# Sparse graph attention: the destination's gathered score accumulates in PSUM onto the source's columns

## The chip, the cores and the metric

The kernel runs on one core of one Trainium2 chip. The metric is the device time of one execution in microseconds; lower is better. The whole network below is one program of some 50,000 instructions, and the change touches one stage of it.

## The reference, cut to what matters

The network takes 3125 node vectors of 256 numbers and two edge lists, and runs two rounds of a graph layer beside an attention layer, each followed by a mixture of experts. The stage that matters is the gate of the first mixture. It is a graph attention (four heads with four numbers each) over 65,536 random edges whose ends are numbers below 4096 (a source beyond the last node counts as the last node, an edge with a destination beyond it drops out), and its result weighs four experts that all nodes run through.

```python
h = (x_flat @ W_gat).reshape(M, HEADS, NUM_EXPERTS)
a_src = (h * att_src).sum(-1)                 # four scores per node
a_dst = (h * att_dst).sum(-1)
e = leaky_relu(a_src[src] + a_dst[dst], negative_slope=0.2)
e_max = segment_max(e, dst)                   # the self loops are among src, dst
ee = exp(e - e_max[dst])
alpha = ee / (segment_sum(ee, dst)[dst] + 1e-16)
agg = segment_sum(h[src] * alpha[:, :, None], dst).reshape(M, 16) + b_gat
scores = layernorm(agg).reshape(M, HEADS, NUM_EXPERTS).mean(1)
# top two of the four scores, softmax over them, and the experts' outputs are weighed by it
out = sum(g[ei] * (gelu(x @ W1[ei] + b1[ei]) @ W2[ei] + b2[ei]) for ei in range(4))
```

The softmax needs a shift per destination, and any shift that is the same for all edges of a destination gives the same result. The kernel takes the self loop's score in place of the maximum, where the scores are near enough to zero (`NEAR`), and has another path, `in_full`, for other data.

## The kernel before, in words

**Buckets.** Earlier stages have sorted the edges into chunks of 128 places. There are 25 destination tiles of 128 nodes, and each has 30 chunks (`CHUNKS`), ordered by the tile of the source node: 750 chunks in all. `low_d` in DRAM holds for each place the low seven bits of the destination (row 0) and of the source (row 1).

**A step.** `sparse()` is a generator that works through the chunks six at a time (`SOME`), 125 steps, and it has four parts:

- `fetched` (L1520) loads the low bits of six chunks, broadcast over 128 partitions, into `hot` (four buffers; L1524), and VectorE turns them into one-hot columns by a comparison with the partition's number (L1525).
- `gathered` (L1535) multiplies, for each chunk, the source one-hot by a table of the source tile (`tables[0]`: 20 columns a node, four `att_s` scores and 16 numbers `hg`, each split into three bfloat16 parts that add up to the float32 value; L1540) and the destination one-hot by a table of the destination tile (`tables[1]`: eight columns a node, four `att_d` scores and four self-loop scores, in three parts; L1542). Both results stand side by side in `pg` (six chunks by three parts by 28 columns of PSUM, two buffers), and VectorE adds the three parts into `vs` (L1544).
- `weighed` (L1547) runs once for two steps, on 12 chunks. VectorE adds the destination's score to the source's (L1550), applies the leaky rectifier (L1551), and subtracts the self-loop score (L1552); ScalarE takes the exponential (L1553); VectorE multiplies the 16 numbers by it (L1555); ScalarE and GpSimd split the result into three bfloat16 parts, `mp3` (L1558 to L1561).
- `put_of` (L1528) builds the destination one-hots the other way round (`put`, three buffers, VectorE, L1531), and `added` (L1566) multiplies them with `mp3` into `acc`, one bank that collects the 30 chunks of a destination tile (L1571); ScalarE copies it to `got` (L1574).

**What runs beside it.** The steps are drawn from the generator while experts 1 and 2, and the last group of expert 0, run: after each output tile of an expert (`keep_beside`, L1608), `each1` = 2.6 steps on average are emitted. An expert's part is a pair of float32 matmuls for each of four hidden blocks (`experts_hidden`, L284) with a Gelu on ScalarE (L287), then four float32 matmuls and a bias row for each of up to four row tiles (`expert`, L1418, L1419), and a ScalarE copy of the result to SBUF (L1611).

**The order.** Each engine runs its instructions in the order that the framework's scheduler has laid down beforehand, by its own model of costs and from the dependencies and the pools' buffer counts. What stands next to what on TensorE, VectorE and ScalarE is therefore decided by it and not by the source alone, and a change of one instruction can move others.

**Before and after the stage.** The groups ahead of it normalise, transpose and project the nodes and run expert 0; the tables are built from `node` and `goal` (L1499 to L1507). After it come the totals (L1629 to L1636), a branch to `in_full`, and expert 3 with the weighing of all four.

Of the kernel before, what the change touches and what calls it, by code (L numbers as in the profile page):

```python
# [8 lines left out]
F32 = mybir.dt.float32  # L9
BF16 = mybir.dt.bfloat16  # L10
I32 = mybir.dt.int32
AF = mybir.ActivationFunctionType
OP = mybir.AluOpType
# [4 lines left out]
P = 128  # L18
N = 3125
D = 256  # L20
NT = 25
# [31 lines left out]
HIS = 25  # L53
# [15 lines left out]
SOME = 6  # L69
# [34 lines left out]
def tile_gps(ctx: ExitStack, tc: tile.TileContext, a, out):  # L104
    nc = tc.nc
    V, S, G, T = nc.vector, nc.scalar, nc.gpsimd, nc.tensor
# [1279 lines left out]
    with ExitStack() as st:  # L1386
# [2 lines left out]
        V.memset(agg, 0.0)  # L1389
        node = fp.tile([P, NT, 20], F32, name="node", tag="node")  # L1390
        V.memset(node, 0.0)
        att_s, hg = node[:, :, 0:4], node[:, :, 4:20]
        goal = fp.tile([P, NT, 8], F32, name="goal", tag="goal")
        att_d = goal[:, :, 0:4]
        xT = xnT
# [27 lines left out]
        with ExitStack() as st2:  # L1423
# [74 lines left out]
            V.scalar_tensor_tensor(self_e, self_e, 0.2, self_e, op0=OP.mult, op1=OP.max)  # L1498
            tables = []  # L1499
            for nm, x, n in (("tabs", node, 20), ("tabd", goal, 8)):  # L1500
                tab = xp.tile([P, NT, 3, n], BF16, name=nm, tag=nm)
                rest = xp.tile([P, NT, n], F32, name=f"{nm}_r", tag="tabr", bufs=1)
                S.activation(tab[:, :, 0, :], x, AF.Copy)
                V.tensor_tensor(rest, x, tab[:, :, 0, :], op=OP.subtract)
                S.activation(tab[:, :, 1, :], rest, AF.Copy)
                V.tensor_tensor(tab[:, :, 2, :], rest, tab[:, :, 1, :], op=OP.subtract)
                tables.append(tab.rearrange("p t k v -> p t (k v)"))  # L1507
            over = buckets.over
            far = small.tile([P, 2], F32, name="far", tag="far")
            V.tensor_reduce(far[:, 0:1], att_s, axis=AX.XY, op=OP.max)  # L1510
# [23 lines left out]

            def gathered(at, vs, k0, n, hot):  # L1535

                pg = ps.tile([P, SOME, 3, 28], F32, name="pg", tag="pg", bufs=2)
                for j in range(n):
                    dh, k = (k0 + j) // CHUNKS, (k0 + j) % CHUNKS
                    T.matmul(pg[:, j, :, 0:20], lhsT=hot[:, 1, j * P:(j + 1) * P],  # L1540
                             rhs=tables[0][:, min(k, HIS - 1)], start=True, stop=True)
                    T.matmul(pg[:, j, :, 20:28], lhsT=hot[:, 0, j * P:(j + 1) * P],  # L1542
                             rhs=tables[1][:, dh], start=True, stop=True)
                V.tensor_reduce(vs[:, at:at + n], pg[:, :n].rearrange("p j k v -> p j v k"), axis=AX.X, op=OP.add)  # L1544
                return k0, n, at

            def weighed(vs, n):  # L1547
                vs = vs[:, :n]
                e = vs[:, :, 0:4]
                V.tensor_tensor(e, e, vs[:, :, 20:24], op=OP.add)  # L1550
                V.scalar_tensor_tensor(e, e, 0.2, e, op0=OP.mult, op1=OP.max)  # L1551
                V.tensor_tensor(e, e, vs[:, :, 24:28], op=OP.subtract)  # L1552
                S.activation(e, e, AF.Exp)  # L1553
                m = vs[:, :, 4:20].rearrange("p j (h v) -> p j h v", h=4)
                V.tensor_tensor(m, m, e[:, :, :, None].to_broadcast([P, n, 4, 4]), op=OP.mult)  # L1555
                mp3 = xp.tile([P, 2 * SOME, 3, 20], BF16, name="mp3", tag="mp3", bufs=4)
                rest = xp.tile([P, 2 * SOME, 20], F32, name="mrest", tag="mrest", bufs=1)
                S.activation(mp3[:, :n, 0], vs[:, :, 0:20], AF.Copy)  # L1558
                G.tensor_tensor(rest[:, :n], vs[:, :, 0:20], mp3[:, :n, 0], op=OP.subtract)
                S.activation(mp3[:, :n, 1], rest[:, :n], AF.Copy)  # L1560
                G.tensor_tensor(mp3[:, :n, 2], rest[:, :n], mp3[:, :n, 1], op=OP.subtract)  # L1561
                return mp3
# [13 lines left out]
            def sparse():  # L1576
# [5 lines left out]
                for i, k0 in enumerate(left):  # L1582
                    nx = fetched(left[i + 1], min(SOME, n - left[i + 1])) if i + 1 < len(left) else None
                    if not i % 2:
                        vs = xp.tile([P, 2 * SOME, 28], F32, name="vs", tag="vs", bufs=2)
                    done.append(gathered(SOME * (i % 2), vs, *x))
                    if i % 2 or not nx:
                        m = weighed(vs, sum(d[1] for d in done))
                        todo += [(m, *d) for d in done]
                        done = []  # L1590
                    if ready:
                        added(*ready.pop(0))
                    if len(todo) > 3:
                        ready.append(put_of(*todo.pop(0)))
                    x = nx
                    yield
# [30 lines left out]
            for _ in beside1:  # L1627
                pass
            tot = xp.tile([P, NT, 20], F32, name="tot", tag="tot")  # L1629
            V.tensor_reduce(tot, got.rearrange("p t (k v) -> p t v k", k=3), axis=AX.X, op=OP.add)  # L1630
            den = tot[:, :, 0:4]
            V.tensor_scalar(den, den, 1.0, 1e-16, op0=OP.add, op1=OP.add)
            V.reciprocal(den, den)
            V.tensor_tensor(tot[:, :, 4:20], tot[:, :, 4:20], hg, op=OP.add)
            V.tensor_tensor(agg.rearrange("p t (h e) -> p t h e", e=4), tot[:, :, 4:20].rearrange("p t (h e) -> p t h e", e=4),
                            den[:, :, :, None].to_broadcast([P, NT, 4, 4]), op=OP.mult)  # L1636

        def in_full(ap, ps):
# [626 lines left out]
```

## Time and profile before

| | us |
|---|---|
| Median of the timed runs | 3667.17 |
| Lowest and highest of three | 3664.85, 3675.57 |
| The profiled execution's own time | 3698.38 |
| Its span in the profile | 3696.6 |
| TensorE matmul busy in the span | 3477.4 (94%) |
| VectorE busy | 1912.1 (52%) |
| ScalarE busy | 1117.6 (30%) |
| GpSimd busy | 915.9 (25%) |
| The stage of the sparse attention: first `pg` matmul to last `acc` matmul | 1915.0 to 2235.5 |

How to read it: the share of an engine is a mean over stages with different limits, and so the stage's own busy times are looked at below. PE is TensorE's matmuls, PEld its weight loads, DVE is VectorE, ACT ScalarE, POOL GpSimd, and SP the queue that issues most transfers. Matmuls are pipelined, so that a row of the profile is longer than the turn that the matmul takes on the engine; L1540 is line 1540 of the kernel. The profiled execution is one, with a time of its own; the times are from other executions.

### The profile page before, as it was taken

The page shows a single profiled execution, that of the slowest core. Times are in us where ns is not written, and L with a number is a line of the kernel's source. Part 1 is how long each engine was busy: PE and PEld are TensorE (multiplying, and loading weights), DVE is VectorE, ACT ScalarE, POOL GpSimd, SP SyncE. Part 2 cuts the span into 40 slices and gives each one's busy share as a digit, 9 for nine tenths or more (in the row PEclk, how much of TensorE's full clock was granted, in tenths as well). Part 3 has the DMA queues.
Part 4 walks back from the last instruction along what each step waited for, and adds up shares of the span by engine and source line. Part 5 has one row for each costly group of instructions (what it writes and reads, how often), then busy time and mean ns, then how long its engine had stood idle before and what let it go on. Part 6 is the DMA issues. An engine that isn't in the chain of part 4 may idle for free. (4 is left out here: it accounts for less than half of the span.)

```text
span 3696.6 us, 50192 instructions
## 1 busy us (share of the span) xinstructions
PE 3477.4 (94%) x18153; PEld 2114.0 (57%) x18153; DVE 1912.1 (52%) x6827; ACT 1117.6 (30%) x2092; POOL 915.9 (25%) x915
## 2 busy tenths in 40 slices
PE   6999999989999899899899898999999999999998
PEld 3666566656566566544466665564444544444687
DVE  8757767777677687110529888761023032223421
ACT  5433433334333443200346774320023000000233
POOL 0044325532455066000003232100024010000244
PEclk9999899999999899999999999999999999999999
DMA  7013525541456276522666661103211222221576
GB/s 216 18 39 43 66 42 55 63 73 32 49 58 65 64 92 71 142 87 87 205 187 167 177 183 52 47 12 115 82 37 47 72 66 61 60 61 51 154 185 154
DMA packets 347439, 326.89 MB, mean 88 GB/s; under 512 B 143792, under 2 KB 311497, under 8 KB 345751
## 3 DMA queue, kind: packets, MB, share of 16 engines
q1 hardware_dynamic: 212503, 280.87, 29.4%
q10 hardware_dynamic: 105424, 26.40, 7.8%
q0 software_dynamic: 29232, 16.09, 2.6%
q8 instruction: 151, 2.47, 0.3%
q14 instruction: 129, 1.06, 0.1%
HBM read 239.75 MB, written 90.83 MB: 89 GB/s over the span
## 5 line engine op out<-in xcount | busy, mean ns | idle before, releaser
L431 POOL DMA_INDIRECT btab<-b_word,b_key x512 | 535.2, 1045 | 674.3 <-PE mm L284 294.2
L1192 PE MATMUL ag<-chb,Hb 128*128 128x512 bf16 (+1 forms) x1800 | 420.8, 388 | 3.8 <-issue 3.8
L1192 PE MATMUL ag<-chb,xb 128*128 128x512 bf16 (+2 forms) x1950 | 401.5, 366 | 10.1 <-DMA xb<-xb_d 5.4
L284 PE MATMUL mm<-hT,w 128*128 128x512 f32 (+1 forms) x896 | 386.6, 570 | 2.0 <-ACT hid L287 1.4
L1092 PE MATMUL o<-w,hid 128*128 128x256 f32 (+1 forms) x1600 | 387.1, 390 | 0.0
L1092 PEld LDWEIGHTS o<-w,hid 128*128 128x128 f32 (+1 forms) x1600 | 293.8, 190 | 54.0 <-issue 14.3
L1192 PEld LDWEIGHTS <-xb 128*128 128x128 bf16 (+1 forms) x2100 | 183.8, 98 | 226.9 <-issue 17.2
L287 ACT ACTIVATE hid<-mm,fm 128x512 f32<-128x512 f32 (+1 forms) x336 | 210.4, 630 | 328.3 <-PE mm L284 326.4
L1192 PEld LDWEIGHTS <-Hb 128*128 128x128 bf16 (+1 forms) x2100 | 184.8, 99 | 217.3 <-issue 25.4
L284 PEld LDWEIGHTS mm<-hT,w 128*128 128x128 f32 x896 | 163.2, 201 | 143.5 <-issue 124.9
L1418 PE MATMUL o<-f0w,hid 128*128 128x256 f32 (+1 forms) x800 | 215.4, 398 | 3.7 <-ACT hid L287 3.7
L950 PE MATMUL mm<-wqkv,hT 128*128 128x512 f32 (+1 forms) x400 | 205.6, 639 | 9.0 <-DVE kmax L961 5.7
L284 PE MATMUL mm<-xnT,f0w 128*128 128x512 f32 (+1 forms) x448 | 204.6, 582 | 4.6 <-issue 4.0
L475 DVE SCALAR_TENSOR_TENSOR b_junk<-kr,b_key,b_tri 128x128 bf16<-128x128 f32 x512 | 175.4, 343 | 33.7 <-DMA kr<-keys_g 31.5
L1809 POOL DMA_INDIRECT slots<-rb,r_ati x50 | 49.4, 987 | 505.3 <-DVE rb L1802 399.8
L732 ACT ACTIVATE g_st<-gc 128x400 bf16<-128x400 f32 x192 | 93.5, 500 | 242.8 <-PE gc L728 239.6
L1418 PEld LDWEIGHTS o<-f0w,hid 128*128 128x128 f32 (+1 forms) x800 | 141.0, 190 | 40.1 <-issue 13.9
L2147 DVE TENSOR_TENSOR a2T<-a2T,ag 128x512 f32<-128x512 f32 x24 | 15.9, 688 | 277.8 <-PE ag L1192 277.7
L719 DVE TENSOR_TENSOR g_ol<-g_all,g_lo 128x1024 bf16<-128x1024 bf16 (+1 forms) x199 | 136.3, 685 | 35.8 <-PE gc L728 34.7
L728 PEld LDWEIGHTS <-g_ol 128*128 128x128 bf16 (+1 forms) x1589 | 119.1, 164 | 61.7 <-issue 42.7
L232 ACT ACTIVATE hT<-tr,fm 128x512 f32<-128x512 f32 (+1 forms) x126 | 85.5, 719 | 159.7 <-PE tr L230 158.4
L1936 POOL DMA_INDIRECT out_dram<-yo,dest x56 | 87.5, 1562 | 186.2 <-DMA out_dram<-yo,dest 78.7
(505 smaller groups left out, 5691.5 us busy)
## 6 DMA issues: line engine op xcount, KB each, us to landing
hot<-low_d SPq DMA_DIRECT2D x125, 384.0 KB
kr<-keys_g SPq DMA_DIRECT2D x256, 128.0 KB
f1w<-in_f_w_dram SPq DMA_DIRECT2D x56, 512.0 KB
slots<-blank SPq DMA_DIRECT2D x14, 1950.0 KB
A<-g_st ACTq DMA_DIRECT2D x24, 800.0 KB
chb<-A SPq DMA_DIRECT2D x48, 397.2 KB
chb<-A SPq DMA_DIRECT2D x48, 384.0 KB
chb<-A SPq DMA_DIRECT2D x120, 128.0 KB
```

The costliest lines, as they stand in the source:

```text
L284: pace[0] = T.matmul(ph[:, :n], lhsT=w1[:, k, hb * P:(hb + 1) * P], rhs=xT[:, k, :n], start=(k == 0), stop=(k == 1))
L287: S.activation(h[:, :n], ph[:, :n], AF.Gelu, bias=bias[hb])
L431: d = G.indirect_dma_start(out=btab.rearrange("(n o) -> n o", o=1), out_offset=bass.IndirectOffsetOnAxis(ap=self.key[:, c:c + 1].bitcast(I ...
L475: ranked = V.scalar_tensor_tensor(junk, kr[:, (j % EACH) * P:(j % EACH + 1) * P], self.key[:, c0 + j:c0 + j + 1], self.tri, op0=OP.is_equa ...
L719: V.tensor_tensor(lo[:r, :, :k], self.all[:r, :, :k], self.lo[:r, None, c:c + k].to_broadcast([r, P, k]), op=OP.is_equal)
L728: T.matmul(p[:, j, :], lhsT=lo[:r, :, j], rhs=hi[:r, j, :h], start=True, stop=True)
L732: S.activation(stage.rearrange("p h (l j) -> p h l j", l=2)[:, :, :, j0:j0 + k], p.rearrange("p j (l h) -> p h l j", l=2), AF.Copy)
L950: pace[0] = T.matmul(pqk[:r], lhsT=hT[:, k, j * P:j * P + r], rhs=wqkv[:, k, 0:512], start=(k == 0), stop=(k == 1))
L1092: pace[0] = T.matmul(po[:r], lhsT=hid[hb][:, j * P:j * P + r], rhs=w2[:, hb, :], start=(hb == 0), stop=False)
L1192: T.matmul(acc[fb, g][:, :n], lhsT=Xb[:r, s, i, fb * P:(fb + 1) * P], rhs=ch[:r, at:at + n], start=first, stop=last, skip_group_check=g == ...
L1418: T.matmul(po[:r], lhsT=hid[hb][:, j * P:j * P + r], rhs=w2[:, hb, :], start=(hb == 0), stop=False)
L1936: d = G.indirect_dma_start(out=out, out_offset=bass.IndirectOffsetOnAxis(ap=dest[:, c:c + 1], axis=0), in_=yo[:, c, :], in_offset=None, bo ...
```

## The change

In `pg`, and so in `vs`, the 28 columns of a chunk become 24. The columns are reordered so that the 16 numbers come first, then the four source scores. The source table is padded with four zero columns to 24 and cleared by a memset, so that the first matmul writes 72 contiguous columns and opens the accumulation. The second matmul, with the destination's eight columns, accumulates onto columns 16 to 23 of each of the three parts: its four scores add to the source's scores, and its four self-loop scores add to the zeros. The addition on VectorE in `weighed` is left out. All else is renumbering.

```diff
-        att_s, hg = node[:, :, 0:4], node[:, :, 4:20]
+        hg, att_s = node[:, :, 0:16], node[:, :, 16:20]
...
-                tab = xp.tile([P, NT, 3, n], BF16, name=nm, tag=nm)
+                whole = xp.tile([P, NT, 3, n + n % 8], BF16, name=nm, tag=nm)
+                tab = whole[:, :, :, 0:n]
+                if n % 8:
+                    V.memset(whole, 0.0)
...
-                tables.append(tab.rearrange("p t k v -> p t (k v)"))
+                tables.append(whole.rearrange("p t k v -> p t (k v)"))
...
-                pg = ps.tile([P, SOME, 3, 28], F32, name="pg", tag="pg", bufs=2)
+                pg = ps.tile([P, SOME, 3, 24], F32, name="pg", tag="pg", bufs=2)
                 for j in range(n):
                     dh, k = (k0 + j) // CHUNKS, (k0 + j) % CHUNKS
-                    T.matmul(pg[:, j, :, 0:20], lhsT=hot[:, 1, j * P:(j + 1) * P],
-                             rhs=tables[0][:, min(k, HIS - 1)], start=True, stop=True)
-                    T.matmul(pg[:, j, :, 20:28], lhsT=hot[:, 0, j * P:(j + 1) * P],
-                             rhs=tables[1][:, dh], start=True, stop=True)
+                    T.matmul(pg[:, j], lhsT=hot[:, 1, j * P:(j + 1) * P],
+                             rhs=tables[0][:, min(k, HIS - 1)], start=True, stop=False)
+                    T.matmul(pg[:, j, :, 16:24], lhsT=hot[:, 0, j * P:(j + 1) * P],
+                             rhs=tables[1][:, dh], start=False, stop=True)
                 V.tensor_reduce(vs[:, at:at + n], pg[:, :n].rearrange("p j k v -> p j v k"), axis=AX.X, op=OP.add)
...
-                e = vs[:, :, 0:4]
-                V.tensor_tensor(e, e, vs[:, :, 20:24], op=OP.add)
+                e = vs[:, :, 16:20]
                 V.scalar_tensor_tensor(e, e, 0.2, e, op0=OP.mult, op1=OP.max)
-                V.tensor_tensor(e, e, vs[:, :, 24:28], op=OP.subtract)
+                V.tensor_tensor(e, e, vs[:, :, 20:24], op=OP.subtract)
                 S.activation(e, e, AF.Exp)
-                m = vs[:, :, 4:20].rearrange("p j (h v) -> p j h v", h=4)
+                m = vs[:, :, 0:16].rearrange("p j (h v) -> p j h v", h=4)
...
-                        vs = xp.tile([P, 2 * SOME, 28], F32, name="vs", tag="vs", bufs=2)
+                        vs = xp.tile([P, 2 * SOME, 24], F32, name="vs", tag="vs", bufs=2)
...
-            den = tot[:, :, 0:4]
+            den = tot[:, :, 16:20]
...
-            V.tensor_tensor(tot[:, :, 4:20], tot[:, :, 4:20], hg, op=OP.add)
+            V.tensor_tensor(tot[:, :, 0:16], tot[:, :, 0:16], hg, op=OP.add)
```

More of the change, by code (lines that the diff above doesn't have):

```diff
@@ L1630, in tile_gps @@
             V.tensor_reduce(tot, got.rearrange("p t (k v) -> p t v k", k=3), axis=AX.X, op=OP.add)
-            den = tot[:, :, 0:4]
+            den = tot[:, :, 16:20]
             V.tensor_scalar(den, den, 1.0, 1e-16, op0=OP.add, op1=OP.add)
             V.reciprocal(den, den)
-            V.tensor_tensor(tot[:, :, 4:20], tot[:, :, 4:20], hg, op=OP.add)
-            V.tensor_tensor(agg.rearrange("p t (h e) -> p t h e", e=4), tot[:, :, 4:20].rearrange("p t (h e) -> p t h e", e=4),
+            V.tensor_tensor(tot[:, :, 0:16], tot[:, :, 0:16], hg, op=OP.add)
+            V.tensor_tensor(agg.rearrange("p t (h e) -> p t h e", e=4), tot[:, :, 0:16].rearrange("p t (h e) -> p t h e", e=4),
                             den[:, :, :, None].to_broadcast([P, NT, 4, 4]), op=OP.mult)
```

## Prediction

> **What bounds the kernel now.** I read the page's slices first, then the busy time of the stage that the change touches, then its groups of instructions, its waits, and two strips of the timeline. The span is 3696.6 us, and TensorE is busy almost throughout.
>
> ```profile
> PE   6999999989999899899899898999999999999998
> DVE  8757767777677687110529888761023032223421
> ```
>
> The edited code runs in one stage, from 1915 us (the first `pg` matmul) to 2235 us (the last `acc` matmul): slices 21 to 24, where both PE and DVE are high. Its stretches (columns: length, then busy us and count for PE, PEld, DVE, ACT, POOL, then clock, DMA share, GB/s):
>
> ```profile
> 1950.00:2050.00 100.00, 95.21 (x977) 62.82 (x976) 92.62 (x214) 66.74 (x130) 31.67 (x42) 1.00 0.69 169
> 2050.00:2200.00 150.00, 134.58 (x1361) 90.82 (x1360) 127.79 (x295) 106.84 (x190) 45.64 (x59) 0.95 0.65 177
> sum 317.00, PE 289.98 PEld 193.94 DVE 269.74 ACT 218.34 POOL 93.72; mean PE 72.49 PEld 48.49 DVE 67.43 ACT 54.58 POOL 23.43
> ```
>
> The sum is over 1915 to 2232. DVE is busy 269.7 of 317 us, 93% in the first 100 us shown and 85% in the next 150. PE shows 290, but a matmul's row is longer than its turn on the engine. These strips show turns as the distance between starts (the first strip is the edited code, the second a later stage with 53 and 512 columns):
>
> ```profile
> 2021.04 0.19 PE L1540 MATMUL pg<-tabs,hot 128*128 128x60 bf16 x1
> 2021.07 0.17 PE L1542 MATMUL pg<-tabd,hot 128*128 128x24 bf16 x1
> 2021.09 0.19 PE L1540 MATMUL pg<-tabs,hot 128*128 128x60 bf16 x1
> ```
>
> ```profile
> 2899.83 0.19 PE L1192 MATMUL agb<-chb,Hb 128*128 128x53 bf16 x1
> 2899.85 0.38 PE L1192 MATMUL ag<-chb,Hb 128*128 128x512 bf16 x1
> 2900.07 0.19 PE L1192 MATMUL agb<-chb,Hb 128*128 128x53 bf16 x1
> ```
>
> So a 60- or 24-column matmul takes a turn of some 26.5 ns, a 53-column one about 25, and 512 columns 215. With the trace's other turns (0.43 us for each of 192 L284 records, 0.216 for 400 of L1418, 0.21 for 50 of L1419, 0.047 for 732 of L1571) PE's own work is 82.6 + 86.4 + 10.5 + 34.4 + 1500 x 0.0265 = 39.8, and some 6 for short tiles: 260 us at full clock, 268 at the mean granted 0.97. PE and DVE thus both have work for 85% of the stage, and neither is saturated. The groups (count, busy us, mean ns, idle before and its releasers) and then the waits (idle us in total, times, longest) say how they hold each other up:
>
> ```profile
> L1525 DVE TENSOR_SCALAR hot<-hot,own 128x1536 bf16<-128x1536 bf16 x121 | 83.9, 694 | 35.6 <-DMA hot<-low_d 34.9
> L1544 DVE TENSOR_REDUCE vs<-pg 128x168 f32<-128x504 f32 x125 | 81.7, 671 | 9.5 <-PE pg L1542 8.8 <-POOL mrest L1559 0.5
> L1553 ACT ACT_TABLE_LOAD x42 | 53.9, 1283 | 0.9 <-DVE vs L1552 0.2
> L287 ACT ACT_TABLE_LOAD x41 | 52.6, 1283 | 0.7
> L1550 DVE TENSOR_TENSOR vs<-vs 128x48 f32<-128x48 f32 x62 | 14.7, 238 | 0.1
> ```
>
> ```profile
> PE pg L1540 <- DVE vs L1544: 12.1, 12, 2.6
> PE acc L1571 <- DVE put L1531: 5.2, 8, 1.8
> PE acc L1571 <- POOL mp L1561: 4.5, 6, 1.2
> PE pg L1540 <- DVE hot L1525: 3.6, 2, 2.5
> ```
>
> PE's waits are for the reduce that frees a `pg` buffer, the compare that makes `hot`, the `put` one-hots, and the weighed chain that ends in `mp`: 25 us, nearly all on DVE's work. DVE in turn waits 34.9 us for `hot` loads, which are issued only when PE has used the buffer four steps earlier. It is one loop of 125 steps, at 317/125 = 2.54 us.
>
> **The change part by part.** *The reduce, L1544.* It reads 432 numbers instead of 504. DVE rows of the same stage give the slope: 192 elements 0.35 us (L1555, median of the tile's list), 504 elements 0.67, so 1.03 ns an element; 72 fewer save 74 ns, and 125 of them 9.3 us.
>
> *The add, L1550, is gone.* 63 rows sum to 15.3 us (62 of the form shown and one half-size of 0.6). DVE rows overlap: the rows of the stage sum to 309.4 us against 269.7 busy, over 619 instructions, 64 ns each. Off the engine comes 15.3 - 63 x 0.064 = 11.3 us. Together DVE loses 20.6 us of 269.7, 0.165 us of each step's 2.16.
>
> *The first matmul streams 72 columns for 60.* Turns of 25 ns at 53 columns and 215 at 512 give 0.41 ns a column, so 12 columns cost 5 ns: 750 x 5 = 3.8 us on PE. If the next weight load, and not the stream, sets the 26.5, it costs nothing. I take half in the path, +2.
>
> *The second matmul accumulates.* The trace shows no 24-column accumulation onto part of a wider result. Below, its price is nothing: `agb` accumulates 53 columns at 25 ns. Above it is the turn of L1571, which accumulates 60 columns onto the same 60 at 47 ns: 20 ns more, 750 times, 15.4 us. L728, which does not accumulate but has the same strided weights as L1571, shows a turn of 62 ns with its 50 columns, so the strided weights explain the 47; I take zero, and gain from accumulation itself is excluded since 26.5 is already near the shortest turn in the trace.
>
> [...]
>
> *The memset of the padded table* (900 words; 500 words took 0.475 us at L1391, so 0.9) moves in the instruction order to the renewal groups near 1840 us, where DVE was busy 19 of 50 us: nothing. Exposed between 1901 and 1906 us, on the chain to the first `pg`, it would cost 0.9. The renumbered columns keep their element counts: nothing.
>
> *The order.* The scheduler lays the stage out anew. GpSimd's order and the 125 loads keep their sequence on SP. Weight loads and the last `y_d` store move by a few places there; that store now follows the branch, ahead of the loads that read it, and waits only for an ACT copy that is long done. After the stage, the centring of `wkv` on DVE (L1382 to L1384) comes a few instructions later, ahead of its first use: nothing. On ACT the alternation of Exp and Gelu breaks less often: 67 table loads in the stage instead of 83, 16 x 1.283 = 20.5 us less. ACT is busy 218 of 317 us, so this only shortens the weighed chain; what PE can get from it is at most the 4.5 us it waits for `mp`, and I take 2. On PE the groups of six accumulates stand nearer to the gathers: 33 of 125 stood seven to nine groups behind, now four do, the rest six. On DVE the weighed chain ends 0.97 reduces after its input on average, formerly 1.40, and `hot` compares lead by up to three instead of four.
>
> [...]
>
> *The sum.* In 1950 to 2050 DVE is the pace, 93% busy, and what it loses comes out in full: 20.6 x 100/317 = 6.5. In the other 217 us it is 85 to 92% busy once the stage has started, and I take half, 20.6 x 217/317 / 2 = 7.0. With +2 for PE and -2 for ACT: -13.5, say -14. The profiled execution took 3698.4 us (span 3696.6), 31 above the median of 3667.2; its span would become about 3683, and the median 3667 - 14 = 3653.
>
> **The rivals.** *The gain is swallowed.* PE's 268 us plus 3.8 is 86% of the stage, and the granted clock was 0.95 in 2050 to 2200. If the loop's pace is PE and its loads there, DVE merely waits longer at `hot`, where it already waits 34.9 us. Against it: PE waits 25 us for DVE's products. Time: between -8 and +4, at 3665.
>
> *Slower: the accumulates come too early.* PE works in order. An accumulate brought forward a group finds its `put` or `mp` unfinished, and the gathers behind it, which issue the next loads, stand too. 29 groups are brought forward. At 1 us each, below the longest waits of such an accumulate now (1.8 and 1.2 us), it costs 29, so 3653 + 29 = 3682. It decides from 14/29 = 0.5 us a group. For it: the smaller distance. Against it: 86 groups already stand at six, and PE's whole wait there is 9.7 us.
>
> *Accumulation costs a longer turn*, the 47 ns above: +15.4 on PE, 3653 + 15 = 3668, no change.
>
> *More than the sum.* If the whole stage followed DVE's pace, 20.6 x 317/270 = 24; with all of `mp`'s 4.5, and 2050 to 2200 running at the 977 records per 100 us of the stretch before it instead of 907 (7% of 150, 10 us): -39, 3628.
>
> **How the numbers follow.** My sum and the "more" case together 0.66, swallowed 0.17, longer turn 0.04, slower by early accumulates 0.13. A measurement of this kernel can tell about 0.3%, 11 us, from no change. So faster 0.66, same 0.21, slower 0.13. The likeliest time is 3653. The range runs from 3628, the far end of the gain, to 3678, which takes in the swallowed case and most of the slower one; about 0.08 is left out on that side and 0.07 below. The forecast's own range is 3628 to 3656.
>
> **What would show it.** Right: the reduce at about 0.596 us, the add gone, 72-column turns near 31 ns and the pair near 58; DVE busy near 249 us in the stage; PE's wait for the reduce well below 12 us; the stage some 14 us shorter, and nothing changed after 2240 us. Swallowed: the wait for `hot` loads above 45 us, with the stage as long as before. Early accumulates: PE's waits at `acc` above 25 us. Longer turn: a pair above 70 ns. The forecast is wrong if the stage does not shorten with the reduce at 0.6 us.

## The result, and the profile after

The changed kernel takes 3682.01 us (median of 12 runs, 3674.38 to 3686.18), the kernel before, on the same chip, 3670.95 us (12 runs, 3664.85 to 3680.11): a ratio of 1.0024, 95% interval 1.0015 to 1.0033. It is slower by a quarter of a per cent, 6 to 12 us; the prediction, 3653 with a range up to 3678, had the wrong sign. The profiled execution of after took 3682.4 us (span 3680.7). Before's profiled execution (span 3696.6) was an unusually long one, 27 us over its median, so the two spans can't be set against each other; the stage can. It is read here from the first `pg` matmul to the start of the last copy of an expert's output (`y`, L1611 before and L1613 after): **321.9 us before, 330.0 after**.

Line numbers in after are two or three higher than in the prediction: L1528 the `hot` compare, L1543 and L1545 the two `pg` matmuls, L1547 the reduce, L1563 the end of the weighed chain, L1573 the accumulates. First the busy time of the stage up to the last `acc` matmul (columns as in the prediction), of before and then of after:

```profile
1915.00:2235.50 320.50, 292.81 (x2938) 195.85 (x2937) 270.57 (x620) 221.01 (x407) 95.43 (x126) 0.97 0.63 166
1898.70:2220.90 322.20, 294.89 (x2922) 199.81 (x2921) 251.83 (x557) 200.42 (x386) 96.73 (x126) 0.96 0.62 164
```

The DVE groups of the same stretch (count, busy us, mean ns, idle before and its releasers):

```profile
L1528 DVE TENSOR_SCALAR hot<-hot,own 128x1536 bf16<-128x1536 bf16 x121 | 80.4, 665 | 34.1 <-DMA hot<-low_d 33.6
L1547 DVE TENSOR_REDUCE vs<-pg 128x144 f32<-128x432 f32 x125 | 74.3, 600 | 29.3 <-PE pg L1545 24.2 <-POOL mrest L1561 4.9
```

The reduce fell from 671 to 600 ns, the add is gone, DVE lost 18.7 us and ACT 20.6: the work went as the prediction's terms said. But DVE now sits 24.2 us waiting for `pg` matmuls, formerly 8.8, and the stretch did not get shorter. The waits in the stage (idle us in total, times, longest) show what became of PE's gain:

```profile
PE acc L1573 <- POOL mp L1563: 14.2, 13, 2.7
PE pg L1543 <- DVE vs L1547: 7.2, 7, 1.7
PE pg L1543 <- DVE hot L1528: 2.4, 5, 0.7
```

The wait for the reduce fell by 4.9 us, and that for `mp` rose by 9.0, from 5.2 in the same stretch of before. With the lesser ones not shown, PE is idle for 27 to 28 us of the stage in both kernels. What changed is where these gaps lie, and that costs clock, as e8 below shows. The longest gap, on PE's timeline (start, duration, idle before in brackets):

```profile
2021.38 0.19 PE L1543 MATMUL pg<-tabs,hot 128*128 128x72 bf16 x1
...
2021.67 0.19 PE L1543 MATMUL pg<-tabs,hot 128*128 128x72 bf16 x1
2021.71 0.17 PE L1545 MATMUL pg<-tabd,hot 128*128 128x24 bf16 x1
2024.56 0.42 PE L1573 MATMUL acc<-mp,put 128*128 128x60 bf16 x6 [2.68 <-POOL mp L1563]
...
2025.10 0.22 PE L1543 MATMUL pg<-tabs,hot 128*128 128x72 bf16 x1
2025.13 0.21 PE L1545 MATMUL pg<-tabd,hot 128*128 128x24 bf16 x1
2025.19 0.22 PE L1543 MATMUL pg<-tabs,hot 128*128 128x72 bf16 x1
```

The accumulate waited 2.68 us for `mp`. Before the gap a pair of gathers takes 58 ns (five of them from 2021.38 to 2021.67), after it 90. Two stretches, before and after 2025.0 (the third number from the end is the granted clock):

```profile
2021.40:2024.80 3.40, 0.72 (x19) 0.67 (x19) 2.86 (x8) 1.21 (x4) 1.82 (x2) 1.00 1.00 209
2025.00:2028.40 3.40, 3.40 (x35) 2.85 (x32) 2.86 (x8) 1.17 (x5) 1.37 (x2) 0.50 0.52 122
```

In this stage the clock falls to half in pieces of 3.4 us, or some few of these in a row. Added up over the stage it was at half for 17.1 us before and for 29.6 us after. Last, the end of PE's timeline, of after and then of before:

```profile
2220.49 0.42 PE L1573 MATMUL acc<-mp,put 128*128 128x60 bf16 x6
2220.76 0.85 PE L284 MATMUL mm<-xnT,f0w 128*128 128x53 f32 x6
2222.85 1.89 PE L284 MATMUL mm<-xnT,f0w 128*128 128x53 f32 x8 [1.24 <-ACT hid L287]
2224.67 3.66 PE L1418 MATMUL o<-f0w,hid 128*53 128x256 f32 x8
```

```profile
2235.21 0.46 PE L1571 MATMUL acc<-mp,put 128*128 128x60 bf16 x6
2235.61 1.07 PE L1418 MATMUL o<-f0w,hid 128*53 128x256 f32 x4
2236.61 0.29 PE L1419 MATMUL o<-rows,ones 3*53 3x256 bf16 x1
```

In the new sequence the small last group of 53 rows still has its hidden blocks and outputs ahead of it when the last accumulate is done: the stage ends 8.0 us after the start of the last `acc` matmul, formerly 1.4.

So there were two theories of the loss: the **sequence** that the scheduler laid out for the changed instructions costs it, by its tail and by gaps that halve the clock; or the **instructions** themselves cost it, the accumulation above all. And one question on the missing gain: what is the pace of the stage, if not DVE?

### The profile page after: what moved, and what is told of

The parts are those of the page before. It is cut to its first block, busy times and chain, and to the rows that moved or that the text cites. A ratio compares the mean times of both kernels' runs of the same rounds, so it can differ in the third digit from the quotient of the medians.

```text
span 3680.7 us, 50131 instructions
## 1 busy us (share of the span) xinstructions
PE 3473.2 (94%) x18153; PEld 2117.0 (58%) x18153; DVE 1895.0 (51%) x6765; ACT 1099.9 (30%) x2076; POOL 916.1 (25%) x915
## 5 line engine op out<-in xcount | busy, mean ns | idle before, releaser
L1192 PE MATMUL ag<-chb,xb 128*128 128x512 bf16 (+2 forms) x1950 | 401.6, 366 | 10.6 <-DMA chb<-A 10.1
L1418 PE MATMUL o<-f0w,hid 128*128 128x256 f32 (+1 forms) x800 | 218.9, 407 | 2.9 <-ACT hid L287 2.8
L475 DVE SCALAR_TENSOR_TENSOR b_junk<-kr,b_key,b_tri 128x128 bf16<-128x128 f32 x512 | 175.4, 343 | 22.5 <-DMA kr<-keys_g 20.5
L1811 POOL DMA_INDIRECT slots<-rb,r_ati x50 | 49.5, 990 | 500.4 <-DVE rb L1804 395.0
L1418 PEld LDWEIGHTS o<-f0w,hid 128*128 128x128 f32 (+1 forms) x800 | 145.1, 195 | 43.9 <-issue 17.2
L1154 POOL TENSOR_TENSOR rest<-h1o,Hb 128x512 f32<-128x512 f32 (+1 forms) x25 | 28.9, 1157 | 419.2 <-ACT Hb L1153 419.2
## 6 DMA issues: line engine op xcount, KB each, us to landing
kr<-keys_g SPq DMA_DIRECT2D x256, 128.0 KB
chb<-A SPq DMA_DIRECT2D x120, 128.0 KB
```

The lines of the kernel that those rows point to most:

```text
L475: ranked = V.scalar_tensor_tensor(junk, kr[:, (j % EACH) * P:(j % EACH + 1) * P], self.key[:, c0 + j:c0 + j + 1], self.tri, op0=OP.is_equa ...
L1192: T.matmul(acc[fb, g][:, :n], lhsT=Xb[:r, s, i, fb * P:(fb + 1) * P], rhs=ch[:r, at:at + n], start=first, stop=last, skip_group_check=g == ...
L1418: T.matmul(po[:r], lhsT=hid[hb][:, j * P:j * P + r], rhs=w2[:, hb, :], start=(hb == 0), stop=False)
```

## The experiments

Times of whole runs differ by chip (before's median was 3671, 3736, 3749, 3695 and 3704 us where it was timed), so each run is set against before on its own chip; and the stage in the profile is read beside it, since it is the finer measure here. In the table "half" is the time at half clock within the stage. "At full clock" is the stage less half of that, which is what PE's work would take there if a matmul takes twice as long at half clock. In the stage of after, L1418's matmuls start 0.216 us apart at full clock and 0.427 at half (medians), but a pair of gathers takes 58 ns and 90, as above: the column is an estimate from the first of these, not a measurement. All are in us; the ratio is to the kernel before, with its 95% interval.

| run | stage | half | at full clock | ratio |
|---|---|---|---|---|
| before | 321.9 | 17.1 | 313.4 | |
| e0 before, again | 320.1 | 10.2 | 315.0 | 1.0021 (1.0001 to 1.0042) |
| after | 330.0 | 29.6 | 315.2 | 1.0024 (1.0015 to 1.0033) |
| e6 after, again | 330.2 | 30.7 | 314.9 | 1.0007 (0.9990 to 1.0024) |
| e1 after's instructions, old sequence | 318.3 | 10.2 | 313.2 | 1.0002 (0.9977 to 1.0028) |
| e14 the same, again | 320.9 | 13.7 | 314.1 | one run |
| e2 before's instructions, new sequence | 336.9 | 39.9 | 317.0 | 1.0033 (1.0013 to 1.0053) |
| e3 before without the add, old sequence | 324.6 | 20.5 | 314.4 | 1.0000 (0.9973 to 1.0026) |
| e4 after, new sequence with the old tail | 327.1 | 27.3 | 313.5 | 1.0012 (0.9996 to 1.0029) |
| e5 after, small group of expert 2 first | 325.6 | 23.9 | 313.7 | 1.0018 (1.0004 to 1.0032) |
| e7 before, small group of expert 2 first | 326.4 | 30.7 | 311.1 | 1.0022 (1.0000 to 1.0044) |
| e8 after, gaps filled | 324.6 | 10.1 | 319.6 | 1.0003 (0.9990 to 1.0016) |
| e9 after's instructions, old sequence, filled | 318.2 | 3.4 | 316.5 | 0.9985 (0.9971 to 0.9998) |
| e10 before, filled | 317.9 | 3.4 | 316.2 | 0.9987 (0.9975 to 1.0000) |
| e11 as e14, light reduce | 311.4 | 6.8 | 308.0 | one run |
| e12 as e14, light matmuls | 309.1 | 48.0 | 285.1 | one run |
| e13 as e14, light loads | 303.6 | 0.0 | 303.6 | one run |
| e15 as e14, five hot buffers | 297.1 | 6.8 | 293.7 | 0.9933 (0.9901 to 0.9964) |
| e16 as e9, five hot buffers | 302.9 | 0.0 | 302.9 | 0.9962 (0.9937 to 0.9987) |
| e17 as e10, five hot buffers | 300.2 | 0.0 | 300.2 | 0.9953 (0.9938 to 0.9967) |

### The same kernels again: e0 and e6

> The kernel before once more, unchanged: ratio 1.000 within 0.1%. It is for a second profile, since the first profiled execution took 3698 us, 28 above the median of its timed runs. Expected: the span near 3670 us, and the 28 us found either ahead of the stage (whose first gathering matmul then starts near 1899 us, as in the changed kernel) or in the stage (which is then shorter than 320 us).

> The changed kernel again, unchanged. Ratio 1.002 to 1.003. If the half-clock windows belong to the sequence (theory C), this profile has 25 us or more of half clock in the stage, at mostly the same places (near 48, 126, 150, 167, 218, 232, 270 us from its start) and the mean clock of its timed runs is 0.001 or so below that of the kernel before; if they fall by chance, 10 to 20 us at other places.

The unchanged kernel against itself gave 1.0021, with 1 just outside its interval: on these chips a ratio means little below 0.2 to 0.3%, and after's 1.0024 of the first chip was 1.0007 on e6's, less than was expected. The stage repeats better: 320.1 for 321.9, and 330.2 for 330.0. The half-clock pieces repeat too. In after five of them begin 47.8, 126.3, 150.2, 167.3 and 218.5 us behind the first `pg` matmul; on e6's chip there are five at 49.5, 128.0, 151.9, 169.0 and 220.2. Four of the five stand just behind a gap of over 1 us on PE, or two of them.

### Sequence or instructions: e1 and e2

Both kernels were given the other's sequence. Behind the stage's code, its instructions on PE, DVE, ACT and SP are chained in a written-out order by dependencies that only order and wait for nothing (GpSimd's order is the same in both); in e2 each add stands right ahead of its rectifier. In the traces PE and ACT run e1 in exactly before's sequence of matmuls and activations, and e2 in after's.

```diff
+for p, q in zip(seq, seq[1:]):
+    tc.add_manual_dep(q, p.name, mybir.DependencyInfo(
+        mybir.DependencyClass.NoSync, mybir.DependencyReason.DATA), reason="pinned")
```

> The changed kernel, with the stage's instructions on TensorE, VectorE, ScalarE and SyncE pinned to the sequence that the kernel before has there (the removed add is simply missing). Theory A, the new sequence is what costs, and the instructions themselves gain: 3655 to 3665 us, a ratio of 0.996 to 0.999 to the kernel before, the stage some 5 to 15 us shorter than before. Theory B, the instructions cost (the 72-column turn, +5 ns times 750 = 4 us, and what VectorE saves is lost in waits): the same or slower than before, 3671 to 3682 us, ratio 1.000 to 1.003.

> The kernel before, with the stage's instructions pinned to the sequence of the changed kernel, each add standing right ahead of its rectifier. Theory A (sequence): slower than the kernel before, and slower than the changed kernel, 3682 to 3700 us, ratio 1.003 to 1.008. Theory B (instructions): as before, 3665 to 3675 us, ratio 0.999 to 1.001, or faster by some us thanks to the 16 fewer table loads.

The stretches of e0, e1 and e2 (columns as above):

```profile
1972.20:2292.30 320.10, 291.85 (x2943) 195.00 (x2941) 269.43 (x621) 221.16 (x409) 98.64 (x126) 0.98 0.63 168
1944.20:2262.50 318.30, 294.19 (x2943) 199.22 (x2942) 251.31 (x558) 221.04 (x409) 100.61 (x126) 0.98 0.65 169
1957.90:2294.80 336.90, 301.45 (x2943) 201.55 (x2941) 278.28 (x625) 202.54 (x393) 93.41 (x126) 0.94 0.64 160
```

The new instructions in the old sequence take 318.3 us (320.9 in e14), no longer than before's 320.1 and 321.9; the old instructions in the new sequence take 336.9. The loss belongs to the sequence. Within one sequence the accumulation is worth 1.4 us of the stage in the old one, on the means of two runs each that differ by 1.8 and 2.6 us among themselves, and not the 5 to 15 us that theory A expected; in the new one it is worth 7 us (336.9 to 330.0), most of it clock. No run pins a kernel to its own sequence and changes nothing else. The nearest is e3 below, whose stage at full clock is 314.4 us where before and e0 have 313.4 and 315.0.

### The add alone: e3

```diff
-                V.tensor_tensor(e, e, vs[:, :, 20:24], op=OP.add)
```

This is before, pinned to its own sequence, leaving out the destination's score.

> The kernel before in its own sequence, with the add L1550 left out: the destination's score is missing from the edge's score. Takes 11 us of engine time from VectorE and nothing else. If VectorE's time sets the stage's pace in this sequence: 4 to 11 us faster, ratio 0.997 to 0.999. If it does not: 0 to 2 us, ratio 0.9995 to 1.0005.

The stretch of its stage (columns as above):

```profile
1960.50:2285.10 324.60, 294.71 (x2943) 197.54 (x2941) 260.06 (x558) 221.34 (x409) 99.53 (x126) 0.97 0.64 165
```

DVE lost 9 us (269.4 in e0, 260.1 here) and the stage did not shorten: 324.6. Its wait for `hot` loads rose from 34.5 us in e0 to 46.0, and in e1 it is 45.7. DVE finishes earlier and waits longer for its next load. That is the sign that the prediction had set for "the gain is swallowed", seen as soon as the sequence is held fixed.

### The tail: e4, e5 and e7

e4 follows after's own sequence up to its 120th step and before's from there. e5 and e7 let the scheduler lay out a new sequence in which expert 2 begins with its small group:

```diff
-    for g in range(NG)
+    for g in (range(NG) if e == 1 else [NG - 1, *range(NG - 1)])
```

> The changed kernel in its own sequence up to step 119 of 125, and from there in the sequence of the kernel before. Theory T (the tail): in the changed kernel the matmuls of the last, 53-row group of expert 2 stand behind the last accumulate, and the stage ends 8.0 us after that accumulate instead of 1.4. Then the tail falls to 1 to 2 us here, the time by 5 to 7 us against the changed kernel, ratio to the kernel before 1.0005 to 1.0015. Theory C (the clock): the loss is in half-clock windows inside the stage (29.6 us of half clock in the changed kernel's profile, 17.1 and 10.2 in two of the kernel before); then the tail's change brings under 3 us, ratio 1.0015 to 1.003.

> The changed kernel with one more edit: expert 2 takes its 53-row group first instead of last, and the scheduler lays the stage out anew. Theory T: no chain of small matmuls is left behind the last accumulate, tail 1 to 2 us, stage 318 to 324 us, ratio to the kernel before 0.998 to 1.0005. Theory C: it depends on the half-clock time of the new sequence alone: with 10 to 17 us ratio 0.998 to 1.000, with 30 us or more 1.001 to 1.003.

> The kernel before with the same further edit as the run with the small group first. The tail of the kernel before is already 1.4 us, so theory T expects nothing from the tail: ratio 0.9995 to 1.0015, the difference to the changed kernel with that edit being what the accumulation is worth in an order that suits both: 2 to 6 us in favour of the accumulation. If the sequence decides by its half-clock windows, the two differ by half of the difference in their half-clock time, whichever way.

With the old tail the stage ends 1.5 us behind the start of the last accumulate, not 8, but that accumulate comes 3.6 us later, as the small group's work has moved ahead of it: 327.1, a gain of 2.9. So 6.5 us of tail were worth less than half of that. The small group first gives 325.6 for after and 326.4 for before, which is a loss for before: its half-clock time went to 30.7 us. At full clock all of these lie between 311 and 315, as does the old sequence: what each of these new sequences loses against the 321.0 of before and e0 is mostly clock, by the estimate of the table. Among themselves they are not told apart by it: e7 has 6.8 us more half clock than e5, by which it should be 3.4 us longer, and it is 0.8 longer.

### Filling the gaps: e8, e9 and e10

If gaps on PE halve the clock, matmuls that do nothing in these gaps should keep it up. Ahead of the places where PE had been idle for long (66 in e8, 71 in e9, 69 in e10) stands

```diff
+warm = ps.tile([P, 512], F32, name="warm", tag="tr", bufs=1)
+T.matmul(warm, lhsT=ident_b, rhs=all6.rearrange("p a b -> p (a b)")[:, 0:512], start=True, stop=True)
```

> The changed kernel in its own sequence, with 66 extra 128x512 bfloat16 matmuls into a bank that the stage doesn't use, put on TensorE right ahead of 15 instructions before which both of its profiles show TensorE idle for over 0.6 us (as many as fit into the shorter of the two gaps at 0.215 us each, 14.2 us in all). They leave the result and every wait alone. Theory C (idle stretches bring half-clock windows, and these cost about half their length): the half clock in the stage falls from 30 us to under 15, the stage from 330 to 321 to 325 us, the time by 5 to 8 us against the changed kernel. Theory W (the waits themselves are the loss, the clock a by-product): the stage stays at 328 to 332 us or grows, since the waits are as long as before.

> The changed kernel in the sequence of the kernel before (its stage took 318.3 us with 10.2 us of half clock), with 71 such filling matmuls at the 17 idle places of that run. Theory C: half clock 0 to 5 us, stage 313 to 317 us, the fastest version, ratio to the kernel before 0.998 to 1.000. Theory W: stage 318 to 322 us, ratio 1.000 to 1.001.

> The kernel before in its own sequence, with 69 such filling matmuls at the 16 places that both of its profiles show idle. Theory C: half clock falls from 10 to 17 us to 0 to 7, the stage from 320 to 322 to 315 to 319 us; the run with the accumulation in the same sequence and filled is then 1 to 4 us shorter, which is what the accumulation itself is worth. Theory W: stage 320 to 324 us.

The stretch of e8's stage (columns as above):

```profile
1904.10:2228.70 324.60, 307.09 (x2998) 204.47 (x3008) 253.64 (x562) 203.29 (x393) 95.74 (x126) 0.98 0.64 165
```

In after the half-clock time fell from 29.6 to 10.1 us and the stage by 5.4. (The whole kernel took 1.0003 of before's time, which this noise can't tell from e6's 1.0007.) That PE's idle gaps bring on the half clock, and that this was much of the stage's loss, is thereby shown by intervention. In the old sequence half fell to 3.4 us, but the stage only to 318, where 313 to 317 were expected of e9: the fillers take turns themselves, and at full clock these stages are 2 to 4.5 us longer than the same without them. e9 and e10 are alike, so even at a steady clock the accumulation brings nothing.

### What is the pace: e11, e12, e13

Three kernels, each with one kind of work made light, all in e1's sequence, beside e14 on the same chip. They leave out what the light work would have computed: two of three parts of the gathered numbers, half of the columns of most of the experts' sums, and half of the loaded bits:

```diff
-V.tensor_reduce(vs[:, at:at + n], pg[:, :n].rearrange("p j k v -> p j v k"), axis=AX.X, op=OP.add)
+V.tensor_reduce(vs[:, at:at + n], pg[:, :n, 0:1].rearrange("p j k v -> p j v k"), axis=AX.X, op=OP.add)   # e11
...
-T.matmul(po[:r], lhsT=..., rhs=w2[:, hb, :], start=(hb == 0), stop=False)
+T.matmul(po[:r, 0:wide], lhsT=..., rhs=w2[:, hb, 0:wide], ...)   # e12: wide = D // 2 for hb > 0, and the hidden blocks alike
...
-hot = xp.tile([P, 2, SOME * P], BF16, name="hot", tag="hot", bufs=4)
+hot = hots[len(loads) % 4]   # e13: four tiles of the same shape, declared once
...
-nc.sync.dma_start(h, low_d[None, :, k0 * P:(k0 + n) * P].to_broadcast([P, 2, n * P]))
+nc.sync.dma_start(h[:, :, :cut * P], low_d[None, :, k0 * P:(k0 + cut) * P].to_broadcast([P, 2, cut * P]))   # e13: cut = 3 for 6, from the fifth load on
```

> The changed instructions in the old sequence, but the reduce reads only the first of the three parts of a chunk (144 numbers for 432); the scores and the weighed values are therefore left incomplete. By the rows of 192 elements (0.35 us) and 432 (0.60 us) a reduce falls to about 0.30 us: DVE loses 0.30 x 125 = 37 us of 251. If DVE is the pace of the stage (the step of the prediction), the stage falls from 318 to between 281 (all of it) and 300 (half). If TensorE's own work is the pace, DVE only waits longer at the hot loads (45.7 us becomes 70 or more), and the stage falls by at most the 10 us that TensorE waits for the reduce: 308 to 318. If the loads are the pace: 315 to 318. To be compared as stage less half of the half-clock time (313.2 in the run of the same sequence before).

> The changed instructions in the old sequence, but with less work for TensorE in experts 1 and 2: of each output's four matmuls three stream 128 columns for 256, and of each hidden block's two the second streams 256 for 512; part of the experts' sums is left out. By the turns of 0.216 and 0.43 us this is at most 300 x 0.108 + 96 x 0.215 = 53 us off TensorE, and at least the 21 of the hidden blocks, if the weight loads (190 ns in their rows) hold the outputs' turns up. If TensorE's own work is the pace: the stage falls from 318 to between 268 and 297. If DVE is the pace (251 us busy, 79% of the stage): 310 to 318, and DVE's waits do not shrink. If the loads are the pace: 310 to 318.

> The changed instructions in the old sequence, but from the fifth on a hot load brings three chunks of numbers for six; the other three chunks keep what was left there, so their gathered values are not those of the reference. A load then moves 192 KB for 384. If the loads are the pace: DVE's 45.7 us of waits for them fall to under 20, and the stage from 318 to 295 or so. If TensorE's own work is the pace: the waits for loads fall, DVE then waits elsewhere, and the stage stays at 312 to 318, since TensorE waits only 3 us for hot. If DVE is the pace: between, 300 to 310.

> The changed instructions in the old sequence once more, on the chip of the three runs above, as what they are compared with. All theories: a stage of 316 to 322 us, 313 to 315 without half of its half-clock time, and DVE's wait for hot loads near 46 us.

The stretches of the four stages, e14 first, then e11, e12, e13 (length, then busy PE, PEld, DVE, ACT, POOL, clock, DMA share, GB/s):

```profile
1961.10:2282.00 320.90, 295.27 (x2943) 199.73 (x2942) 249.20 (x558) 221.24 (x408) 99.16 (x126) 0.98 0.65 167
```

```profile
1962.90:2274.30 311.40, 290.33 (x2943) 198.24 (x2941) 220.46 (x558) 221.11 (x409) 95.04 (x126) 0.99 0.66 172
```

```profile
1958.60:2267.70 309.10, 262.48 (x2943) 195.95 (x2942) 248.82 (x558) 220.48 (x409) 98.39 (x126) 0.92 0.66 173
```

```profile
1970.00:2273.60 303.60, 288.80 (x2943) 196.81 (x2942) 250.08 (x558) 220.08 (x408) 100.68 (x126) 1.00 0.41 98
```

e11: the reduce fell to 296 ns and DVE by 28.7 us; the stage fell by 9.5, a third of it, and the wait for loads rose from 50.6 to 63.3 us. DVE is not the pace. e12: PE's busy time fell by 33 us, and the stage by 11.8. PE's idle time rose from 26 to 47 us and the half clock from 13.7 to 48, which is why the granted clock reads 0.92; at full clock the stage would have lost 29, by the estimate of the table. By the same estimate some 50 us of work were taken off PE, of which 21 came back as waits and 17 as clock. The 309.1 lies in no theory's range; the 285.1 at full clock lies in that of PE. e13 was the surprise: no matmul and no DVE instruction is changed, and the stage falls by 17.3 us with not a moment at half clock. Of the theories only "DVE is the pace" had a range with 303.6 in it, and e11 speaks against that one; for the loads being the pace 295 was expected, for PE 312 or more. The wait for loads still stood at 29.6 us, where under 20 was the sign of the loads. What the half-sized load shortens is the way round the ring: a buffer freed by the gathers, the load issued, landed, compared, gathered. Four steps take 10.0 us in e14 (median, from a step's first gather to that of the step four later) and 9.3 in e13. Of this 0.17 us comes from something else than the size: a load that overwrites three chunks waits only for the gathers of these three, and not of all six.

### The ring: e15, e16, e17

The ring has four buffers. SyncE's waits in e14 say what its next load waits for (idle us, times, longest):

```profile
SPq L1598 <- PE pg L1616: 133.7, 84, 4.5
SPq L1598 <- PE acc L1644: 79.4, 24, 6.8
```

For two thirds of the stage the next load waits for PE, which has not yet got past the gathers that hold the oldest buffer, or the accumulates that stand near them. The trace shows how directly: in e14 the issue of a load ends 0.39 us (median) behind the last gather of the step four earlier. One more buffer lets each load go out a step earlier, and leaves all work and every engine's sequence alone:

```diff
-hot = xp.tile([P, 2, SOME * P], BF16, name="hot", tag="hot", bufs=4)
+hot = xp.tile([P, 2, SOME * P], BF16, name="hot", tag="hot", bufs=5)
```

> The changed instructions in the old sequence, with five buffers for hot instead of four and nothing else changed; every engine's sequence is that of e1. A load can then be issued one step earlier. If the turnaround of the loads (buffer freed by TensorE, load issued, landed, compared) makes the gaps on TensorE, as the half-sized loads suggest: DVE's wait for loads falls from 50 us to under 25 (with 24 in the whole of TensorE's idle time), the half-clock time from 13.7 us to 0 to 7, the stage from 320.9 to between 303 and 312, and the time against the kernel before to 0.996 to 0.999. If the bytes of a load and not the turnaround held it up (the stage moves 167 GB/s): the wait only shifts, and the stage stays at 316 to 321.

> e15 with the 71 filling matmuls of e9. If the loads' turnaround makes the gaps: little is left to fill, and the fillers only cost (71 x 0.2 = 15 us where they find no gap): stage 308 to 318. If not: as e9, 316 to 319.

> The instructions of before in their own sequence, with five buffers for hot and the 69 filling matmuls of e10, to be set against e16: the same but for the accumulation. If DVE becomes the pace once the loads are early, the 20 us of DVE that the accumulation saves show: this stage is 5 to 15 us longer than that of e16. If TensorE's own work is the pace: within 3 us of it.

The stretch of e15's stage, and its waits:

```profile
1927.20:2224.30 297.10, 288.68 (x2943) 197.80 (x2942) 247.67 (x558) 220.18 (x408) 97.21 (x126) 0.99 0.69 181
```

```profile
DVE hot L1599 <- DMA hot<-low_d: 19.4, 21, 2.1
PE pg L1614 <- DVE vs L1618: 2.8, 2, 2.0
PE acc L1644 <- POOL mp L1634: 1.3, 2, 0.9
```

The stage falls by 23.8 us from e14's, more than was expected, and the whole kernel to 0.9933 of before (3681.06 against 3703.78 us, interval 0.9901 to 0.9964): the best version of the study, faster than both kernels. PE is busy 288.7 of 297.1 us; its waits for the reduce and for `mp` have all but gone, though neither the reduce nor the weighed chain is changed. They were the late loads, handed on. SyncE still waits 191 us for PE, since a load still goes out 0.39 us behind the last gather of the buffer's step; but this is now the step five earlier, and DVE's wait for loads fell from 50.6 to 19.4 us. So it is DVE's wait that shows whether the ring is too short, and not SyncE's. The transfers of the stage now run at 181 GB/s, above e14's 167, so bytes did not hold them up. The stages of e16 and e17:

```profile
1923.90:2226.80 302.90, 300.22 (x3014) 203.04 (x3013) 248.16 (x558) 220.75 (x409) 96.55 (x126) 1.00 0.68 176
1931.40:2231.60 300.20, 297.74 (x3012) 199.46 (x3011) 266.14 (x621) 220.29 (x408) 98.82 (x126) 1.00 0.68 178
```

With the fillers (e16) the stage is 5.8 us longer than without: there is little left to fill. e17, before's instructions with DVE at 266 us, takes 300.2 where e16 with DVE at 248 takes 302.9; the ratios, 0.9953 and 0.9962, agree within their intervals. With the ring out of the way 18 us of DVE change nothing, and the accumulation is still worth nothing. That PE is then the pace is argued from its 97% and from so little idle time; no run made PE's work lighter at five buffers.

A fifth buffer in a sequence that the scheduler lays out itself was not tried.

## Why the prediction was wrong

**The costs of the instructions held.** The reduce took 600 ns for 596 predicted; DVE lost 18.7 us in the stage for 20.6; the 72-column matmul's pair takes some 58 ns as predicted, so "accumulation costs a longer turn" (a pair above 70) is out; ACT lost 20.6 us for 20.5. The cleared table's memset took 0.8 us at 1788 us, 110 us ahead of the first `pg` matmul, and delayed nothing that shows.

**The step that failed is the share on the path, in the sum.** "In 1950 to 2050 DVE is the pace, 93% busy, and what it loses comes out in full", and half of it elsewhere: 13.5 us. Measured within one sequence: e3, 9 us of DVE, nothing; e1 and e14 against before and e0, about 19 us, 1.4; e11, 29 us more, 9.5. A busy share of 93% was taken for a pace; the test would have been which wait ends last at PE's gaps and what stands behind it. The prediction had named it: DVE waits 34.9 us for loads "which are issued only when PE has used the buffer four steps earlier. It is one loop of 125 steps". In this ring DVE waited out most of what it saved, all 9 us in e3 and 19 of 29 in e11, the greater part of it at its loads, while one buffer more took 24 us off the stage (e15) and left PE busy for 97% of it.

**The second step that failed is the order**, priced as a gain of 2 us for the fewer table loads and at nothing for all else. It cost some 10: with the same instructions the stage is 330.1 us on the mean of after and e6, and 319.6 on that of e1 and e14. The whole change cost 9.1, from 321.0 on the mean of before and e0. Of these 9.1 us about 8.3 are half of the half-clock time that is added (30.2 less 13.7 us, halved), by the estimate of the table; at full clock the stages differ by 0.9, less than before and e0 do. PE's idle time did not change; its arrangement did. The prediction saw the clock (0.95 in 2050 to 2200) and used it as a constant.

**The rivals.** "The accumulates come too early" came nearest: its 3682 is the time measured, and its mechanism, gathers standing behind an accumulate that waits for `mp`, is what the strip above shows. But its own sign was PE waiting above 25 us at `acc`; all waits there came to 16.2 us, from about 10, and were paid for by shorter ones at `pg`. The price came through the clock and the tail, which it did not name. That its number is the measured one is luck: it held it for a reason that was half right. "The gain is swallowed" describes the old sequence (its sign, above 45 us for loads, is met in e1, e3 and e14), but in after itself the wait was 33.6 us, and the stage longer. "Nothing changed after 2240 us" can't be told from these traces, as the stretch behind the stage differs by 9.6 us between after and e6, which are the same kernel, and the one ahead of it by 76.

**What stays open.** How much of the quarter of a per cent holds on other chips: e6 gave 0.07%, within the noise that e0 shows. And the exact rule by which the clock falls. Gaps over 1 us are as many in before (12, and 10 in e0) as in after (11, and 10 in e6), but in after 8 of the 11 have a half-clock piece begin within 8 us and in e6 6 of the 10, in before 5 of the 12 and in e0 2 of the 10; in e12 one piece has no gap over 0.59 us in the 7 us ahead of it. The traces tell more when a stage is cut into the windows of 3.41 us that the last section finds. In the twenty traces there are 33 windows at full clock with 1.9 us of PE idle or more, and a window at half clock follows all 33; it follows 27 of 55 with 1.3 to 1.9 us, and 17 of 1664 with less. (The bounds were chosen on these same windows, and the ends of matmuls are modelled, so they are rough.) Windows with 1.3 us or more idle are 6 in before and 4 in e0, but 9 in after and 7 in e6. So the new sequence gathers the same idle time into more windows that are poor in work; how the scheduler comes to that was not looked into.

## What to carry to other kernels

A high busy share does not make an engine the pace of a loop that turns over a few buffers (VectorE was at 93% here for 100 us, and 9 us less of it in e3 shortened nothing): ask who waits for the buffer to come free, and try one buffer more before making any member's work shorter. Where a scheduler lays out the order, price the new order as a change of its own, and test it by running the old instructions in the new order and the other way round. When time moves and no engine's work did, look at the granted clock within the stage, piece by piece.

## What was not expected of the hardware

The granted clock of PE falls to half for pieces of 3.4 us, mostly behind idle gaps of 1 to 3 us, and in after and e6 five of these pieces stand at the same places of the sequence on two chips; over the whole kernel it is at half for 237 to 321 us. In after the pieces named above begin 78.5, 23.9, 17.1 and 51.2 us apart, which is 23, 7, 5 and 15 times 3.41: they lie on a grid, and its step is the length of one such piece. No gap ahead of these pieces was longer than 2.68 us, and some were two gaps of about 1.2 us. What the traces show to count is the idle time of a window, as above.

The clock makes PE's time depend on how its idle time is cut up: 66 matmuls that do nothing, put into the gaps, brought half-clock time from 29.6 to 10.1 us and the stage down by 5.4; and 33 us less of busy matmuls shortened a stage by only 12.

The padded, accumulating pair of gathers cost no more than two separate matmuls but for the 5 ns of its twelve columns. From the first matmul's start to the second's it is 32 ns at full clock, formerly 27; from the second's, which accumulates, to the next first's it is 26 ns in both (medians; 58 ns a pair, formerly 53). Accumulating in PSUM onto a strided part of a wider result shows no price of its own in these traces.
